# Inputs of a spectral mixer made chunk by chunk inside the attention ahead of it

## The chip, the cores and the metric

The kernel runs on one core of a Trainium2 chip. The metric is device time in microseconds (us) of one execution, the median of several runs. Profile times are us from the start of the profiled execution's span.

## The reference, cut to what matters

The network has four layers over 2 batches of L = 56·56 = 3136 tokens with C = 128 channels, all float32. Layers 0 and 1 are selective scans. The change lies in layer 2, which adds an attention without a token's own key, and then a spectral mixer; both read a layer norm of the tokens t.

```python
t = t + attn(_ln_t(t))                      # softmax(q q^T / sqrt(128)), diagonal masked
t = t + mix(_ln_t(t), sigma, phi, M_u, M_phi_plus, M_phi_minus, log_weights, gumbel)
t = t + attn3(_ln_t(t)); t = t + experts(_ln_t(t))          # layer 3

def mix(x, ...):                            # x: (2, 3136, 128)
    outs = []
    for i, frac in enumerate((1, 2, 4, 8)):
        xi = x[:, :T // frac]
        si = spectral(xi, sigma, phi, M_phi_plus[i], M_phi_minus[i]) + ar(M_u[i], xi)
        outs.append(pad(si, T))
    w = one_hot(argmax(y)) - y + y          # y = softmax(log_weights + gumbel), 4 values
    return sum(outs[i] * w[i])

def ar(Mu, u):                              # the direct part: three lags
    return sum(shift(u, i) @ Mu[i] for i in range(3))
# spectral: 16 causal convolutions of u with the filters phi, for u and for u with
# alternating signs; each result times sigma^0.25 and a 128x128 matrix, summed
```

## The kernel before, in words

Tokens stand in SBUF as X, 112 tokens of a tile on the partitions, 28 tiles, 2 batches. A chunk (CH = 448) is four such tiles; there are 7 a batch and 14 in all. Layers 0 and 1 run in an order written out by hand. Everything behind them is ordered by a list scheduler, which lists each engine's instructions from the program's dependences; instructions then run in that order on each engine's queue. DMAs are issued by SyncE (SP), in order. Pools decide where a tile lies, and a tile placed where another was waits for the other's last reader.

**Attention 2** (`Attention2.run`, which calls `Attend.run`). Its keys, queries and values are made during the tail of layer 1. For each chunk of queries it steps j over 25 tiles of keys: a matmul for the scores (L1031, tile sc), the exponential on ScalarE (L1033, e), their sum over tiles on GpSimd (L1044, total), and two steps behind, the product with the values (L1025, av). At the chunk's end av is copied (L1056, by), turned by four matmuls (L1060), and added to X divided by the sum of weights (L1067, L1070). `Attend.run` calls a hook `also(at, j)` in each step; attention 3 uses it to make its own inputs, attention 2 passes none.

**The mixer** (`layer2_mixer`, `Mixer`). Its convolutions are products of blocks of 128 tokens. It wants tokens backward, and even and odd tokens apart: tile x is 128 partitions × 13 blocks × both batches' channels, for one parity. So behind attention 2 it

1. computes the routing weights wt and ws from four numbers (L1487 to L1514), some 25 small instructions;
2. makes U, the layer norm of all of X, in four pieces (`layernorm_all`, L77 to L84);
3. reverses the 28 tiles' tokens by matmuls with a reversed identity `anti` (L1529, prv), copies them out (r) and stores them in a DRAM array `back` (L1532);
4. sums the matrices M_u by the routing weights to wu (`stretch_sums`, L1616 and L1618), turns U into channels uT (L108, pt) and computes the direct part into A by three matmuls for each of 8 segments of 392 tokens a batch (L1546, par);
5. loads the filters' taps H (L1366) and windows wA to wD (L1376), and in `Mixer.inputs` the blocks x from `back` with strided rows (L1320, L1322), and forms differences of blocks t, vA, vC and vD on VectorE (L1326 to L1357), with the tiles u0 and S as scratch;
6. runs 32 units. Each has convolution products (L1397, tile cv), of which ScalarE copies (L1412) or VectorE adds (L1410) the results into u0, u1 and S, and projections with matrices Wm (L1582, pj), added to A with a stride of two tokens (L1588). Between units 16 and 17 `Mixer.inputs` is called for the other parity.

**Attention 3** is built ahead of the mixer: five small loads (Wq, Wk, Wv, bq, bv) and a chain of small matmuls and VectorE copies make its constants (L1137 to L1148).

Of the kernel before, what the change touches and what calls it, by code (L numbers as in the profile page):

```python
# [14 lines left out]
F32 = mybir.dt.float32  # L15
BF16 = mybir.dt.bfloat16
AF = mybir.ActivationFunctionType
# [4 lines left out]
B = 2  # L22
# [97 lines left out]
class Scans:  # L120
# [177 lines left out]
    def run(self):  # L298
        with ExitStack() as ctx:
            self.open(ctx)  # L300
            with self.k.tc.manual_schedule():
                self.all_steps()
# [770 lines left out]
class Attention2:  # L1073
# [26 lines left out]
            k.evacuate(self.uT[b][:, CH * c : CH * (c + 1)], pt)  # L1100
            key_tiles(k, bank(self.pp, "pt"), self.uT[b], self.V[b], c)

    def run(self, early):
        k = self.k
        with k.pool("a2") as sp:
            skip = sp.tile([KT, KT], F32, name="skip")
            k.nc.vector.tensor_scalar(skip, k.ident, -1.0, 1.0, ALU.mult, ALU.add)
            done = early()
            with ExitStack() as ctx:
                Attend(k, ctx).run(self.uT, self.uT, self.V, 128.0**-0.5, k.ident, skip=skip)  # L1110
        return done


# [117 lines left out]
HL = L // 2  # L1231
REST = HL - KB * NB
PW = KB + HL + 16

# [48 lines left out]
    return raw, win  # L1285


class Mixer:


# [3 lines left out]

    def __init__(self, k, ctx, back, raw, win):
        self.k, self.back, self.raw, self.win = k, back, raw, win
        sp = ctx.enter_context(k.pool("mixx", 1))
        self.wp = ctx.enter_context(k.pool("mixw", 1))  # L1300
        self.cp = ctx.enter_context(k.pool("mixc", 1))
        self.p1 = ctx.enter_context(k.pool("pconv", 6, psum=True))

        self.x = sp.tile([KB, NB + 1, B * C], F32, name="x")
        k.nc.gpsimd.memset(self.x[:, NB, :], 0.0)
        self.sp = sp
        self.H = self.wp.tile([KB, 2, 2, HL], F32, name="H")
        self.W, self.waiting = {}, None

    def inputs(self, par):  # L1310

        nc, x, back = self.k.nc, self.x, self.back

        def rows(r0, n, more):
            return bass.AP(back.tensor, back.offset + r0 * B * C, [[2 * B * C, n], *more, [1, B * C]])

        for j in (8, 4, 0, NB):
            r0 = L - 1 - 2 * (KB * (NB - j) - 1) - par
            if j < NB:
                nc.sync.dma_start(x[:, j : j + 4, :], rows(r0, KB, [[2 * KB * B * C, 4]]))  # L1320
            else:
                nc.sync.dma_start(x[KB - REST :, NB, :], rows(0 if par else 1, REST, []))  # L1322
        self.v = {f"x{i}": x[:, NB - 1 - i, :] for i in range(NB)}

        def less(out, a, b):
# [143 lines left out]
        self.waiting = None  # L1469


def layer2_mixer(k, d, A, raw, win):

    nc, tc, X = k.nc, k.tc, k.X
    NF = 16
    QC = HL // 4  # L1480
    with ExitStack() as ctx:
        sp = ctx.enter_context(k.pool("m2", 1))

        lw = sp.tile([128, 4], F32, name="lw")
        gu = sp.tile([128, 4], F32, name="gu")
        sg = sp.tile([128, NF], F32, name="sg")
        nc.sync.dma_start(lw, d["L2_log_weights"].partition_broadcast(128))  # L1487
        nc.sync.dma_start(gu, d["L2_gumbel"].partition_broadcast(128))
        nc.sync.dma_start(sg, d["L2_sigma"].partition_broadcast(128))
        nc.scalar.activation(sg, sg, AF.Sqrt)  # L1490
        nc.scalar.activation(sg, sg, AF.Sqrt)
        s = sp.tile([128, 4], F32, name="s")
        nc.vector.tensor_add(s, lw, gu)
        mx = sp.tile([128, 1], F32, name="mx")
        nc.vector.tensor_reduce(mx, s, AX.X, ALU.max)
        nc.vector.tensor_scalar(s, s, mx, None, ALU.subtract)
        nc.scalar.activation(s, s, AF.Exp)
        nc.vector.tensor_reduce(mx, s, AX.X, ALU.add)
        nc.vector.reciprocal(mx, mx)
        nc.vector.tensor_scalar(s, s, mx, None, ALU.mult)  # L1500
        nc.vector.tensor_reduce(mx, s, AX.X, ALU.max)
        hard = sp.tile([128, 4], F32, name="hard")
        nc.vector.tensor_scalar(hard, s, mx, None, ALU.is_equal)
        free = sp.tile([128, 1], F32, name="free")
        nc.gpsimd.memset(free, 1.0)
        for i in range(4):
            nc.vector.tensor_mul(hard[:, i : i + 1], hard[:, i : i + 1], free)
            nc.vector.tensor_sub(free, free, hard[:, i : i + 1])
        wt = sp.tile([128, 4], F32, name="wt")
        nc.vector.tensor_sub(wt, hard, s)  # L1510
        nc.vector.tensor_add(wt, wt, s)
        ws = sp.tile([128, 4, NF], F32, name="ws")
        for i in range(4):
            nc.vector.tensor_scalar_mul(ws[:, i, :], sg, wt[:, i : i + 1])  # L1514

        dp = ctx.enter_context(tc.tile_pool(name="m2d", bufs=1, space=bass.MemoryType.DRAM))
        back = dp.tile([L, B, C], F32, name="back")
        with k.pool("m2u", 1) as up, k.pool("m2b", 3) as bp, k.pool("pm2", 2, psum=True) as pp:
            U = up.tile([TP, NT, B, C], F32, name="U")
            layernorm_all(k, U)  # L1520
            anti = up.tile([TP, TP], F32, name="anti")
            nc.gpsimd.memset(anti, 0.0)
            nc.gpsimd.affine_select(
                out=anti, in_=anti, pattern=[[1, TP]], compare_op=ALU.not_equal, fill=1.0, base=1 - TP,
                channel_multiplier=1,
            )
            for j in range(NT):
                ps = pp.tile([TP, B * C], F32, name="prv")
                nc.tensor.matmul(ps, lhsT=anti, rhs=U[:, j].rearrange("p b c -> p (b c)"), start=True, stop=True)  # L1529
                r = bp.tile([TP, B * C], F32, name="r")  # L1530
                k.evacuate(r, ps)
                nc.sync.dma_start(back[L - TP * (j + 1) : L - TP * j].rearrange("p b c -> p (b c)"), r)  # L1532

            mu = up.tile([128, 4, 3, C], F32, name="mu")
            nc.sync.dma_start(mu, d["L2_M_u"].rearrange("i s d e -> d i s e"))
            wu = up.tile([128, 4, 3, C], F32, name="wu")
            stretch_sums(nc.vector, wu, mu, lambda i: wt[:, i : i + 1])
            uT = up.tile([128, 2 + L], F32, name="uT")
            for b in range(B):
                nc.gpsimd.memset(uT[:, 0:2], 0.0)  # L1540
                tokens_to_channels(k, pp, lambda c0: uT[:, 2 + c0 : 2 + c0 + CH], lambda j: U[:, j, b, :])
                for t0 in range(0, L, QC):
                    r = stretch(t0)
                    ps = pp.tile([128, QC], F32, name="par")
                    for lag in range(3):
                        nc.tensor.matmul(  # L1546
                            ps, lhsT=wu[:, r, lag, :], rhs=uT[:, 2 + t0 - lag : 2 + t0 - lag + QC],
                            start=lag == 0, stop=lag == 2,
                        )
                    k.evacuate(A[:, b, t0 : t0 + QC], ps)  # L1550

        mixer = Mixer(k, ctx, back, raw, win)
        tp = ctx.enter_context(k.pool("tmix", 1))
        wp = ctx.enter_context(k.pool("wmix", 4))
        p2 = ctx.enter_context(k.pool("pproj", 2, psum=True))
# [53 lines left out]
def stretch(t0):  # L1609

    return 0 if t0 < L // 8 else 1 if t0 < L // 4 else 2 if t0 < L // 2 else 3


def stretch_sums(engine, out, m, weight):

    engine.tensor_scalar_mul(out[:, 3], m[:, 0], weight(0))  # L1616
    for i in range(1, 4):
        engine.scalar_tensor_tensor(out[:, 3 - i], m[:, i], weight(i), out[:, 4 - i], ALU.mult, ALU.add)  # L1618
# [233 lines left out]
def program(tc, d, out):  # L1852
    with ExitStack() as ctx:
        k = Chip(ctx, tc)
        dp = ctx.enter_context(tc.tile_pool(name="m2t", bufs=1, space=bass.MemoryType.DRAM))
        with k.pool("big") as bp:
            big = [bp.tile([128, NKT * C if i in (3, 5) else L], F32, name=f"big{i}") for i in range(6)]
            attention = Attention2(k, big)
            with ExitStack() as ctx1:
                heads = []  # L1860

                def follow(ctx):
                    heads.append(Layer1(k, ctx1, d, big))
                    return heads[0].start(ctx)

                layer0(k, d, big, follow)
                heads[0].run(attention.start)
            taps = attention.run(lambda: mixer_filters(k, d, dp))
        with ExitStack() as ctx3:
            attention = Attention3(k, ctx3, d)  # L1870
            A = ctx3.enter_context(k.pool("mixed")).tile([128, B, L], F32, name="A")
            layer2_mixer(k, d, A, *taps)
            attention.run(A)
        layer3_experts(k, d, out)

# [16 lines left out]
```

## Time and the profile before

| | us |
|---|---|
| median of three runs | 9403.43 (9399.32 to 9412.42) |
| the profiled execution | 9399.84 |
| its span | 9398.0 |
| PE busy in the span | 8136.1 (87%) |
| DVE busy | 7072.4 (75%) |
| POOL busy | 6320.6 (67%) |
| ACT busy | 3832.5 (41%) |

In the profile PE is TensorE's matmuls, PEld its weight loads, DVE VectorE, ACT ScalarE, POOL GpSimd. A row of the timeline has start, duration, engine, line, operation, out<-in, shapes and count, and in brackets the idle time before it and what ended it. A row of a group has busy time and mean ns of one behind the first bar, idle time and its releasers behind the second. A float32 matmul mostly appears as two records, a transpose as one. Attention 2 fills 6070 to 6633, the convolutions run from 6768 to about 8500, attention 3 to 9153, and the experts to the end.

### The profile page before, as it was taken

To read this page: it belongs to the slowest core of one execution; us is meant where nothing else is said; L and a number is where in the kernel's file an instruction comes from. 1 tells how busy PE (TensorE), PEld (TensorE's weight loads), DVE (VectorE), ACT (ScalarE), POOL (GpSimd) and SP (SyncE) were. 2 spreads that over 40 slices of the span, in tenths; PEclk is the share of its full clock that TensorE was granted. 3 is DMA by queue.
4 is the path that set the end of the run, shared out by engine and by line. 5 is a ranking of instruction groups with operands and counts; after the bars stand their busy time and mean duration, and the time that the engine had idled before them with its cause. 6 is when DMAs were issued, how large, how long until landed. Compare 5 with 4: busy or idle time off the path is not lost. (4 is left out here: it accounts for less than half of the span.)

```text
span 9398.0 us, 94099 instructions
## 1 busy us (share of the span) xinstructions
PE 8136.1 (87%) x28803; PEld 4794.3 (51%) x28803; DVE 7072.4 (75%) x7442; ACT 3832.5 (41%) x6517; POOL 6320.6 (67%) x4006
## 2 busy tenths in 40 slices
PE   7888888888888888888888888699799999999997
PEld 3444445444444444444444444355488888874545
DVE  8999998999996997997898799600467676665432
ACT  4555545555545555554555555233211111114331
POOL 5999997999995996997899699666211111115550
PEclk9999999999999998998999899699899999999998
DMA  5666664666663884885787588100233333310004
GB/s 156 221 221 216 213 202 136 220 221 215 214 202 104 223 214 121 223 219 146 193 218 202 141 223 213 51 1 1 73 95 107 101 104 94 105 53 1 1 12 147
DMA packets 800676, 1367.59 MB, mean 146 GB/s; under 512 B 125373, under 2 KB 434366, under 8 KB 800138
## 3 DMA queue, kind: packets, MB, share of 16 engines
q1 hardware_dynamic: 800170, 1361.57, 50.3%
q8 instruction: 228, 3.74, 0.2%
q14 instruction: 278, 2.28, 0.1%
HBM read 1320.14 MB, written 41.11 MB: 145 GB/s over the span
## 5 line engine op out<-in xcount | busy, mean ns | idle before, releaser
L423 POOL TENSOR_TENSOR p<-h,c 128x784 f32<-128x784 f32 x2048 | 3759.6, 1860 | 234.5 <-PE acc L371 158.1
L371 PE MATMUL acc<-p,ident 128*128 128x392 f32 x8192 | 3127.5, 513 | 87.4 <-POOL p L423 85.8
L351 DVE TENSOR_TENSOR_SCAN h<-a,state,h 128x784 f32<-128x784 f32 x1536 | 2798.5, 1842 | 88.5 <-ACT a L332 74.0
L371 PEld LDWEIGHTS acc<-p,ident 128*128 128x128 f32 x8192 | 1517.8, 197 | 1175.3 <-POOL p L423 199.5
L410 DVE TENSOR_TENSOR h<-du,b 128x784 f32<-128x784 f32 x1408 | 1336.4, 949 | 176.8 <-PE b L357 174.8
L332 ACT ACTIVATE a<-delta,L0A 128x784 f32<-128x784 f32 x1024 | 939.3, 919 | 836.7 <-DVE h L351 835.0
L426 POOL TENSOR_TENSOR h<-du,b 128x784 f32<-128x784 f32 x640 | 1189.6, 1859 | 3.1 <-DMA b<-rows 3.1
L357 PE MATMUL b<-three,sel 96*128 96x512 bf16 (+1 forms) x2816 | 709.2, 333 | 550.3 <-DVE h L410 509.7
L332 ACT ACTIVATE a<-delta,L1A 128x784 f32<-128x784 f32 x1024 | 937.3, 918 | 534.3 <-DVE h L351 531.9
L1044 POOL TENSOR_TENSOR total<-total,e 128x448 f32<-128x448 f32 (+1 forms) x644 | 729.9, 1133 | 322.3 <-ACT e L1033 294.5
L351 DVE TENSOR_TENSOR_SCAN h<-a,h 128x784 f32<-128x784 f32 x512 | 902.0, 1780 | 40.2 <-ACT a L332 32.3
L1441 POOL TENSOR_TENSOR u<-u,S 128x1024 f32<-128x1024 f32 x64 | 150.1, 2368 | 1136.2 <-DVE S L1410 1136.2
L1410 DVE TENSOR_TENSOR u<-u,cv 128x512 f32<-128x512 f32 x1024 | 623.4, 682 | 342.9 <-PE cv L1397 341.6
L357 PEld LDWEIGHTS <-sel 96*128 96x128 bf16 x2816 | 275.8, 98 | 1158.8 <-issue 921.9
L1033 ACT ACTIVATE e<-sc 128x448 f32<-128x448 f32 (+1 forms) x700 | 380.8, 544 | 788.8 <-PE sc L1031 611.1
L1412 ACT COPY u<-cv 128x512 f32<-128x512 f32 x256 | 149.6, 587 | 849.5 <-PE cv L1397 775.1
L1582 PE MATMUL pj<-u,Wm 128*128 128x196 f32 (+8 forms) x1536 | 351.4, 381 | 5.7 <-DVE A L1588 5.7
L1056 DVE COPY by<-av 128x448 f32<-128x448 f32 x28 | 17.5, 625 | 440.7 <-PE av L1025 440.7
L1031 PE MATMUL sc<-big 128*128 128x448 f32 (+1 forms) x700 | 323.8, 548 | 12.5 <-ACT e L1033 12.5
L385 PE MATMUL acc<-big,ident 128*128 128x392 f32 x384 | 250.6, 784 | 92.3 <-ACT big L391 92.3
L1031 PE MATMUL sc<-q,u 128*128 128x448 f32 (+1 forms) x700 | 323.0, 546 | 0.2 <-DVE q L984 0.2
L1025 PE MATMUL av<-e,big 128*128 128x448 f32 (+1 forms) x700 | 320.7, 544 | 1.1 <-DVE e L1038 1.1
(394 smaller groups left out, 10706.5 us busy)
## 6 DMA issues: line engine op xcount, KB each, us to landing
c<-rows SPq DMA_DIRECT2D x1024, 392.0 KB, 4.0
c<-rows SPq DMA_DIRECT2D x2048, 196.0 KB, 4.4
b<-rows SPq DMA_DIRECT2D x320, 392.0 KB, 4.5
b<-rows SPq DMA_DIRECT2D x640, 196.0 KB, 4.4
H<-raw SPq DMA_DIRECT2D x32, 1568.0 KB, 6.6
wC<-win SPq DMA_DIRECT2D x64, 576.0 KB, 5.9
wA<-win SPq DMA_DIRECT2D x64, 384.0 KB, 5.5
wD<-win SPq DMA_DIRECT2D x64, 320.0 KB, 4.4
```

The lines of the kernel that those rows point to most:

```text
L332: self.k.nc.scalar.activation(x["a"], g["delta"][ci], AF.Exp, scale=self.w["A"](g["kd"], ci, x["n"]))
L351: self.k.nc.vector.tensor_tensor_scan(h, a, h, start, ALU.mult, ALU.add)
L357: self.k.nc.tensor.matmul(ps[:, c0:c1], lhsT=self.w["selB"](x["n"]), rhs=x["g"]["three"][:, c0:c1], start=True, stop=True)
L371: nc.tensor.matmul(job["acc"][:, i, 0:392], lhsT=self.k.ident, rhs=x["p"][:, 392 * i : 392 * (i + 1)], start=False, stop=n == NS - 1,)
L410: nc.vector.tensor_tensor(one["h"], one["g"]["du"][one["ci"]], one["b"], ALU.mult)
L423: nc.gpsimd.tensor_tensor(now["p"], now["h"], now["c"], ALU.mult)
L426: nc.gpsimd.tensor_tensor(three["h"], three["g"]["du"][three["ci"]], three["b"], ALU.mult)
L1031: nc.tensor.matmul(ps[:n], lhsT=keys[b][:, KT * j : KT * j + n], rhs=q, start=True, stop=True)
L1033: nc.scalar.activation(e[:n], ps[:n], AF.Exp, scale=scale)
L1044: nc.gpsimd.tensor_tensor(total[:n], total[:n], e[:n], ALU.add)
L1410: nc.vector.tensor_tensor(place(o), place(o), ps, ALU.add)
L1582: nc.tensor.matmul(ps[:, lo - c0 : hi - c0], lhsT=Ws[f][:, eo, r, :], rhs=u[:, b, f, lo - a0 : hi - a0], start=f == 0, stop=f == 1,)
```

## The change

The mixer's inputs are made chunk by chunk in attention 2's hook. A new class `MixerInputs` holds the pools, the routing weights, wu, tile x and a DRAM array `odd`. It is constructed ahead of attention 2, so the weights and wu come there. For the chunk of queries finished before, the hook calls four steps during the next chunk:

- at j = 4 `tokens`: the layer norm of the chunk's four tiles (Um);
- at j = 11 `channels`: four transposes and one VectorE copy which reads the result backward, so uT holds channels with the tokens reversed;
- at j = 14 `blocks`: for each parity, transposes of every second column of uT, 128 tokens a block. Even blocks are copied into x; odd ones into a tile r (two buffers), and from there into DRAM `odd`, 64 KB a store, 26 stores;
- at j = 18 `direct`: three matmuls per segment (60 in all) on reversed channels, and a copy into A that reads backward.

The last chunk's four steps stand behind attention 2. `Mixer.inputs` loads nothing for even tokens, and x from `odd` in four loads for odd ones. The layer norm of all tokens, the `anti` matmuls, the array `back` and the loads from it are gone. uT lies in a tile `pair`, which takes the places of two tiles of layers 0 and 1. A and the new tiles are taken from the other side of SBUF, and attention 3's constants are built once the tiles of layers 0 to 2's attention are released. The bodies of `products`, `into`, `unit`, `project` and the rest of `Mixer` stay as they are.

```diff
-    def run(self, early):
+    def run(self, early, inputs):
         k = self.k
-        with k.pool("a2") as sp:
+        done = early()
+        with k.pool("a2") as sp, ExitStack() as ctx:
...
-            done = early()
-            with ExitStack() as ctx:
-                Attend(k, ctx).run(self.uT, self.uT, self.V, 128.0**-0.5, k.ident, skip=skip)
+            att = Attend(k, ctx)
+
+            def also(at, j):
+                steps = {4: inputs.tokens, 11: inputs.channels, 14: inputs.blocks, 18: inputs.direct}
+                if at > 0 and j in steps:
+                    steps[j](lambda: att.bank("lo"), *divmod(at - 1, NCH))
+
+            att.run(self.uT, self.uT, self.V, 128.0**-0.5, k.ident, skip=skip, also=also)
+            for step in (inputs.tokens, inputs.channels, inputs.blocks, inputs.direct):
+                step(lambda: att.bank("lo"), B - 1, NCH - 1)
         return done
...
+class MixerInputs:
+    T0 = 2 * KB * (NB + 1) - 1
+    def __init__(self, k, ctx, early, d, A, uT):
+        sp = ctx.enter_context(k.pool("mixx", side="right"))
+        self.up = early.enter_context(k.pool("mixu", 2, side="right"))
...
+        self.odd = dp.tile([KB, NB + 1, B * C], F32, name="odd")
         self.x = sp.tile([KB, NB + 1, B * C], F32, name="x")
-        k.nc.gpsimd.memset(self.x[:, NB, :], 0.0)
+        nc.gpsimd.memset(uT[:, 0 : self.T0 + 1 - L], 0.0)
+        nc.gpsimd.memset(uT[:, self.T0 + 1 :], 0.0)
...
+    def tokens(self, bank, b, c):
...
+        layernorm_tokens(self.k, self.U, self.k.X[:, 4 * c : 4 * (c + 1), b, :], sq, st, C)
+
+    def channels(self, bank, b, c):
+        k = self.k
+        ps = bank()[:, 0:CH]
+        for i in range(4):
+            k.nc.tensor.transpose(ps[:, TP * i : TP * (i + 1)], self.U[:, i, :], k.ident[:TP, :TP])
+        end = self.T0 + 1 - CH * c
+        k.nc.vector.tensor_copy(self.uT[:, end - CH : end], ps[:, ::-1])
+
+    def blocks(self, bank, b, c):
+        k, nc = self.k, self.k.nc
+        i0, i1 = CH * c // (2 * KB), NB + 1 if c == NCH - 1 else CH * (c + 1) // (2 * KB)
+        for par in range(2):
+            ps = bank().rearrange("p (i c) -> p i c", c=C)
+            for i in range(i0, i1):
+                at = self.T0 - 2 * KB * (i + 1) + 2 - par
+                nc.tensor.transpose(ps[:, i - i0, :], self.uT[:, at : at + 2 * KB - 1 : 2], k.ident)
+            for i in range(i0, i1):
+                j = NB if i == NB else NB - 1 - i
+                if par == 0:
+                    k.evacuate(self.x[:, j, C * b : C * (b + 1)], ps[:, i - i0, :])
+                else:
+                    r = self.up.tile([KB, C], F32, name="r")
+                    k.evacuate(r, ps[:, i - i0, :])
+                    nc.sync.dma_start(self.odd[:, j, C * b : C * (b + 1)], r)
+
+    def direct(self, bank, b, c):
+        k, nc = self.k, self.k.nc
+        ps = bank()
+        edges = sorted({CH * c, CH * (c + 1)} | {t for t in (L // 8, L // 4, L // 2) if CH * c < t < CH * (c + 1)})
+        for t0, t1 in zip(edges, edges[1:]):
+            for lag in range(3):
+                end = self.T0 + 1 - t0 + lag
+                nc.tensor.matmul(
+                    ps[:, CH * (c + 1) - t1 : CH * (c + 1) - t0], lhsT=self.wu[:, stretch(t0), lag, :],
+                    rhs=self.uT[:, end - (t1 - t0) : end], start=lag == 0, stop=lag == 2,
+                )
+        nc.vector.tensor_copy(self.A[:, b, CH * c : CH * (c + 1)], ps[:, 0:CH][:, ::-1])
...
     def inputs(self, par):
...
-        for j in (8, 4, 0, NB):
-            r0 = L - 1 - 2 * (KB * (NB - j) - 1) - par
-            if j < NB:
-                nc.sync.dma_start(x[:, j : j + 4, :], rows(r0, KB, [[2 * KB * B * C, 4]]))
-            else:
-                nc.sync.dma_start(x[KB - REST :, NB, :], rows(0 if par else 1, REST, []))
+        if par:
+            for j in (8, 4, 0, NB):
+                js = slice(j, min(j + 4, NB + 1)) if j == NB else slice(j, j + 4)
+                nc.sync.dma_start(x[:, js], self.odd[:, js])
...
+                    A = ctx3.enter_context(k.pool("mixed", side="right")).tile([128, B, L], F32, name="A")
+                    with ExitStack() as early:
+                        given = MixerInputs(k, ctx2, early, d, A, pair[:, 0:MU])
+                        taps = attention.run(lambda: mixer_filters(k, d, dp), given)
+                attention = Attention3(k, ctx3, d)
+                layer2_mixer(k, d, given, *taps)
```

## The prediction

> **What bounds the kernel now.** I read the page's rows of busy time and slices first (TensorE 87%, VectorE 75%), then the busy time by stretch around the change. The columns are PE, PEld, DVE, ACT, POOL, the granted clock, the DMA share and GB/s.
>
> ```profile
> 6100.00:6640.00 540.00, 534.55 (x1561) 270.98 (x1559) 48.12 (x147) 181.51 (x334) 360.63 (x323) 0.99 0.01 2
> 6640.00:6660.00 20.00, 4.59 (x18) 3.27 (x18) 19.56 (x31) 7.47 (x9) 6.32 (x2) 0.59 0.02 6
> ...
> 6700.00:6720.00 20.00, 19.76 (x81) 12.37 (x80) 5.32 (x10) 3.96 (x8) 2.81 (x3) 1.00 0.26 76
> 6720.00:6740.00 20.00, 8.25 (x26) 4.40 (x24) 1.14 (x2) 1.46 (x3) 0.00 (x0) 0.82 0.54 188
> 6740.00:6760.00 20.00, 7.25 (x25) 6.08 (x26) 8.96 (x14) 0.00 (x0) 0.00 (x0) 0.58 0.76 204
> 6760.00:6780.00 20.00, 12.30 (x46) 10.11 (x45) 12.24 (x19) 3.81 (x7) 0.00 (x0) 0.74 0.00 1
> 6780.00:6800.00 20.00, 20.00 (x95) 17.65 (x94) 17.14 (x29) 2.93 (x5) 1.24 (x1) 1.00 0.44 105
> ```
>
> Attention 2 (to 6640) is bound by PE: 534.55 of 540 us busy, with VectorE at 9%, ScalarE at 34%, GpSimd at 67%. From 6780 the mixer is bound by PE too. Between them no engine leads for long: normalization on DVE, then reversal and direct part on PE, then loads and sums. The timeline gives that gap its ends and its last steps.
>
> ```profile
> 6632.90 0.60 DVE L1070 SCALAR_TENSOR_TENSOR X<-pr,r,X 112x128 f32<-112x128 f32 x2
> ...
> 6750.93 0.43 DVE L1330 SCALAR_TENSOR_TENSOR t<-x 128x256 f32<-128x256 f32 x1 [24.05 <-DMA x<-back]
> ...
> 6767.88 0.68 DVE L1326 TENSOR_TENSOR vD<-S 128x512 f32<-128x512 f32 x1
> 6768.05 2.05 ACT L1412 COPY u<-cv 128x512 f32<-128x512 f32 x4 [39.28 <-DVE vD L1326]
> ```
>
> X is final at 6633.50, and the convolution stream runs from 6768.05, when ScalarE may write u0, the scratch of the vD sums. So 134.6 us lie between: to 6728.8 for making U, its reversal and the direct part, to 6750.9 for the loads (x last), 17.1 us for sums on DVE.
>
> **The change, part by part.** *The gap goes.* Only the last chunk's steps stay behind attention 2. Normalizing four tokens' columns took about 5.7 us in attention 3 (DVE 0.69, 0.16, 0.68, ACT 0.63, DVE 0.67, a table load of 1.28, 0.30, DVE 0.20, POOL 1.04, the queue order being the same); then transposes 0.6, reversed copy 0.6, six block transposes and copies about 2, three direct matmuls 2.3: 11.2 us, to about 6644.7. Attention 3's constants now come here. The load of Wq waits on SP for memory that the last direct matmul reads, so about 6646, and the taps H and windows wA to wD are queued behind it. Before, 7.7 MB landed in 22.6 us (6728.3 to 6750.9: 343 GB/s); without x it is about 6.0 MB, 17.5 us, so about 6664. DVE needs 17.1 us from 6645 for t and the v tiles, and its copies of Wq, Wk, M, Mb and vb stand between these and wait for PE (that chain took 6.4 us before, 6631.9 to 6638.3; I add 4): 6666. Both paths meet at about 6666, 32.5 us after X. Saved: 134.6 − 32.5 = **102 us**. The reversed copy has no row as a copy; the scans of line 351, half of which read backward, have minimum, median and maximum of 1822, 1844 and 1868 ns, so I charge a plain copy.
>
> *Attention 2 gets longer, since PE has no idle time there.* These rows size what it gains:
>
> ```profile
> L1546 PE MATMUL par<-uT,wu 128*128 128x392 f32 x96 | 35.7, 512 | 0.0
> L1529 PE MATMUL prv<-U,anti 112*112 112x256 f32 x56 | 22.4, 510 | 28.8 <-DVE r L64 15.5 <-POOL U L84 12.9 <-ACT r L68 0.4
> ...
> L108 PE MATMUL pt<-ident,U 112*128 112x112 f32 x56 | 9.1, 300 | 0.9 <-ACT uT L68 0.9
> ```
>
> The 48 direct matmuls of 392 columns took 35.7 us, 0.74 each; one of 448 in attention's steady pace takes 0.75. For each of 13 chunks: three direct, 2.25; four transposes, 0.60 (the row of line 1207 below); 46 block transposes over 13 chunks at 0.15 each, 0.53. That is 3.38 × 13 = 44 us, and 1 for chunks cut at 392, 784 and 1568. Block transposes read every second column: no row has that for a transpose. The nearest are the accumulations of line 385, at stride 56, 784 ns against 513 in line 371, so the 46 cost between nothing and 4 more (7 if they double). I take nothing. The multiplications by `anti` (22.4 us) fall away inside the gap and are not counted again.
>
> Each chunk also inserts a Sqrt among ScalarE's exponentials. Attention 3 already does so:
>
> ```profile
> 8594.16 1.28 ACT L82 ACT_TABLE_LOAD   x1
> 8595.46 0.30 ACT L82 ACTIVATE st<-st,eps 112x4 f32<-112x4 f32 x1
> 8595.77 1.28 ACT L1033 ACT_TABLE_LOAD   x1
> 8597.07 0.55 ACT L1033 ACTIVATE e<-sc 128x448 f32<-128x448 f32 x1
> ...
> 8597.21 0.60 PE L1207 MATMUL pr<-ident,U 112*128 112x112 f32 x4 [0.69 <-POOL U L84]
> ```
>
> From the load to the next exponential's end is 3.46 us, and PE lost 0.69, not to ScalarE but to U. In attention 2 the queue has scores made ahead, and I count 3.0 us of PE work before PE needs that exponential, against 3.46 less the overlap in which it starts early: 0 to 0.7 a chunk, I take 0.5, so 6 us. A rule speaks against this. The Trainium skill, "ScalarE: Activation LUTs", section "What ACT_TABLE_LOAD costs", adds about 1380 ns of drain to the 1283 ns, 2.66 us a switch. The rows have the 1283 and no drain: 8594.16 + 1.28 meets the Sqrt at 8595.46. By the rule, two switches take 2.76 us more, 13 times: 36 us more, and the gain would shrink to about 9. I keep the row. Attention 2: **+51 us** (42 to 87 between the ends).
>
> Other engines: normalization, the reversed copies and block copies add some 6 us a chunk to DVE (9% busy), 3 of copies and squares to ScalarE (34%), 1 to POOL (67%). PE covers them; if it did not, a chunk would lose what DVE or POOL is late, 1 to 3 us, 13 to 39 in all. The 26 stores of odd blocks have SP to themselves; with two r buffers the third in a row waits for a landing, 2.4 us by the median of back<-r, off PE's path unless an exponential stands behind it.
>
> *The routing weights and wu move ahead of attention 2*, into layer 1's tail: 27 more DVE instructions. Their price depends on GpSimd:
>
> ```profile
> 6647.56 0.16 DVE L1507 TENSOR_TENSOR hard<-hard,free 128x1 f32<-128x1 f32 x1
> ...
> 6647.85 3.02 DVE L1508 TENSOR_TENSOR free<-free,hard 128x1 f32<-128x1 f32 x1
> ```
>
> Alone it is 0.16 us, beside a long multiply of POOL 3.02. In the tail small DVE instructions had means of 0.2 to 0.86, and DVE was busy 99.74 of 151 us, with one idle stretch of 7.7 us for PE. 23 small ones at 0.35 are 8, four wu 2.4 to 7.2; half lies in idle time: **+5** (−5, when they fill waits and the order shifts, to +16). With them go four loads on SP (three small ones, and mu with 786 KB, issued during a scan) and two short memsets on POOL: I count nothing; if the scan's next rows waited behind mu, 3 us.
>
> *Odd tokens at the half-way switch*: x comes from a different array in as many loads of the same bytes: nothing, ±2. *Projection weights* now load behind wD and may be late for the first projection: **+1** (0 to 8).
>
> The sum: −102 + 51 + 5 + 1 = **−45**, on the profiled execution's 9399.84: 9354.8. The median of the runs is 3.6 higher; carried over, 9358. I say 9357.
>
> **The rivals.** *Table switches stall PE.* As worked out, 36 us more: 9393, no change that shows. For it: attention 2 has 1.60 us a step against 1.9 in attention 3, so less cover. Against: no drain in the rows.
>
> *The start of the stream gives it back.* H waits behind Wq, which waits for the last direct matmul and for room; if H, windows and projection weights come one after another with DVE's copies waiting for PE, the stream starts 15 to 25 us later: about 9378. For it: SP is one queue, in order. Against: bytes at 343 GB/s don't need it.
>
> *Slower: layer 1's tail.* Each of the 27 DVE instructions is caught behind a POOL multiply of 2 to 3 us, in the stretch 5919 to 6070, where DVE leads into attention 2. At 3.02 each it is 82 us where I have 5: +32, 9434. It breaks even at 50 us, 1.85 each, and shows as slower from about 2.5 each. For it: the row above, and POOL busy 87.5 of those 151 us. Against: the tail's own small ones averaged under 0.9.
>
> *The change does not do what it says*: a scheduler could leave the hooks' steps behind attention. The order of the instructions shows them inside, so little is left to this: 9400.
>
> **How the numbers follow.** The sum as worked out 0.73; table switches 0.09 (9393); late stream 0.10 (9378); slower tail 0.05 (9434); no effect 0.03. The likeliest gives 9357. The unknowns of the sum (+36 or −9 in attention 2, ±10 in the tail, ±8 at the start) spread it over about 9328 to 9380, and the late stream and part of the switches bring the upper end to 9395. About 0.2% (18.8 us) is what a measurement here can tell from no change: faster takes the first case and most of the late stream, 0.83; same the switches, no effect and edges, 0.11; slower 0.06.
>
> **What would show it.** Right: chunks of attention 2 (starts of line 1056) about 43.5 us apart, not 40; PE waiting under 1 us a chunk; the first u copy about 33 us after X's last update; small DVE instructions before attention 2 under 1 us, and its first exponential near 6075, not 6070. Wrong: chunks of 46 or more with PE waiting for e; H issued well after the last direct matmul, or PE idle 50 us behind attention; attention 2 starting 30 us or more later.

## The result, and the profile after

Three jobs compared the changed kernel with the kernel before. The ratios are 0.9936 (95% interval 0.9919 to 0.9953; medians 9345.87 and 9406.91 us), 0.9945 (0.9932 to 0.9959) and 0.9949 (0.9937 to 0.9962): faster by 0.5 to 0.6%, 49 to 61 us between medians. The profiled execution took 9347.92 us with a span of 9345.7, 52 us less than before.

Busy time by stretch, with the columns of the prediction's first fence:

```profile
6100.00:6640.00 540.00, 539.90 (x1659) 280.38 (x1658) 99.40 (x233) 213.74 (x382) 354.57 (x312) 1.00 0.01 3
6640.00:6680.00 40.00, 39.01 (x120) 19.86 (x118) 5.36 (x15) 15.46 (x28) 26.24 (x24) 1.00 0.01 4
6680.00:6700.00 20.00, 9.45 (x25) 5.61 (x26) 13.17 (x29) 3.01 (x6) 1.23 (x2) 0.60 0.19 55
6700.00:6720.00 20.00, 17.61 (x70) 14.52 (x70) 14.41 (x24) 3.81 (x7) 0.26 (x1) 0.81 1.04 303
6720.00:6740.00 20.00, 16.94 (x64) 13.71 (x63) 13.29 (x25) 2.93 (x5) 7.22 (x6) 0.83 0.53 138
6740.00:6760.00 20.00, 20.00 (x127) 18.71 (x127) 18.16 (x32) 0.37 (x1) 6.29 (x4) 1.00 0.36 93
```

Attention 2 now fills PE wholly, and lasts longer. From 6680 to 6740 PE is idle for 16 of 60 us; before, it was short of work from 6640 to 6780, but for the direct part in between. The timeline shows the same steps as before:

```profile
6679.98 1.13 DVE L1070 SCALAR_TENSOR_TENSOR X<-pr,r,X 112x128 f32<-112x128 f32 x4
...
6694.65 0.62 DVE L1398 COPY A<-lo 128x448 f32<-128x448 f32 x1 [1.05 <-PE lo L1394]
...
6695.19 0.41 DVE L1434 SCALAR_TENSOR_TENSOR t<-x 128x256 f32<-128x256 f32 x1
...
6703.52 1.19 PE L1501 MATMUL cv<-H,t 128*128 128x256 f32 x2 [2.39 <-DMA H<-raw]
...
6710.60 0.68 DVE L1430 TENSOR_TENSOR vD<-S 128x512 f32<-128x512 f32 x1
6710.77 2.05 ACT L1516 COPY u<-cv 128x512 f32<-128x512 f32 x4 [18.27 <-DVE vD L1430]
```

X is final at 6681.11, and the stream runs from 6710.77: 29.7 us, where it was 134.6. And what PE does for the mixer inside attention 2, from the groups of 6110 to 6660:

```profile
L1394 PE MATMUL lo<-pair,wu 128*128 128x448 f32 (+5 forms) x108 | 29.9, 422 | 0.0
...
L1377 PE MATMUL lo<-ident,pair 128*128 128x128 f32 x46 | 7.5, 280 | 0.0
L1365 PE MATMUL lo<-ident,Um 112*128 112x112 f32 x52 | 7.1, 259 | 0.0
```

In all three the idle time before them is zero, and PE is busy for 539.90 of 540 us: no new wait of any size stands in front of it. Five marks, the same in every kernel, cut the span into stages. "Tail" runs from the end of the last scan to attention 2's first exponential; "clock-up" from there to the first copy of av; then to X's last update; to the first u copy; and to the copy of `rest`, which ends the first unit. All in us, from one trace each:

| trace | last scan ends | tail | clock-up | attention 2 | gap | first unit | span behind the scan |
|---|---|---|---|---|---|---|---|
| before | 5919.9 | 150.1 | 39.7 | 523.8 | 134.6 | 43.9 | 3478.1 |
| before, again | 5916.4 | 151.1 | 39.7 | 523.8 | 134.6 | 43.6 | 3478.7 |
| changed | 5922.2 | 153.7 | 39.7 | 565.5 | 29.7 | 48.3 | 3423.5 |
| changed, 2nd | 5921.5 | 155.2 | 42.0 | 565.4 | 29.8 | 48.3 | 3429.0 |
| changed, 3rd | 5928.2 | 154.1 | 42.2 | 565.5 | 29.9 | 46.5 | 3426.9 |
| all steps behind | 5934.2 | 155.2 | 42.0 | 524.0 | 95.7 | 45.3 | 3448.1 |
| no direct part | 5927.3 | 160.5 | 39.7 | 535.1 | 27.6 | 44.3 | 3393.3 |
| switch at the rule's price | 5919.7 | 150.6 | 42.3 | 598.9 | 31.6 | 43.4 | 3454.3 |
| taps first | 5926.5 | 155.2 | 42.0 | 565.4 | 41.9 | 48.0 | 3441.2 |
| weights held back | 5933.2 | 152.8 | 41.6 | 567.5 | 27.5 | 46.6 | 3424.3 |
| late, weights held | 5917.5 | 152.8 | 41.5 | 560.9 | 26.0 | 47.6 | 3417.3 |
| late | 5928.4 | 155.4 | 41.9 | 556.6 | 26.0 | 46.6 | 3417.1 |

From the means of two and three traces: tail +3.7, clock-up +1.6, attention 2 +41.7, gap −104.8, first unit +4.0, what is left +2; together −52.

### The profile page after: what moved, and what is told of

It is laid out like the page before. It is cut to its first block, busy times and chain, and to the rows that moved or that the text cites. A ratio compares the mean times of both kernels' runs of the same rounds, so it can differ in the third digit from the quotient of the medians.

```text
span 9345.7 us, 94244 instructions
## 1 busy us (share of the span) xinstructions
PE 8131.6 (87%) x28823; PEld 4793.0 (51%) x28823; DVE 7098.7 (76%) x7517; ACT 3857.7 (41%) x6560; POOL 6325.3 (68%) x4013
## 4 chain that ended last, share of the span: by engine, by line
PE 49%; DVE 21%; issue 12%; ACT 9%; POOL 4%; DMA 4%; SPq 1%; DVEq 0%; POOLq 0%; ACTq 0%
PE cv L1501 12%; DVE h L351 10%; PE acc L371 7%; DVE h L410 7%; PE av L1025 6%; PE sc L1031 6%; PE pj L1615 4%; ACT a L332 3%; PE b L175 3%; PE acc L385 2%; DMA c<-rows 2%; POOL p L423 2%; DMA whole<-rows 1%; PE pcv L452 1%; PE b L357 1%
## 5 line engine op out<-in xcount | busy, mean ns | idle before, releaser
L1545 POOL TENSOR_TENSOR u<-u,S 128x1024 f32<-128x1024 f32 x64 | 150.1, 2366 | 1043.3 <-DVE S L1514 1043.3
L1025 PE MATMUL av<-e,V 128*128 128x448 f32 (+1 forms) x700 | 320.8, 545 | 0.0
L970 DVE TENSOR_REDUCE m<-lo 112x1 f32<-112x448 f32 x392 | 227.2, 618 | 119.0 <-PE lo L966 118.6
```

The lines of the kernel that those rows point to most:

```text
L1025: nc.tensor.matmul(acc, lhsT=V[b][:n, j, :], rhs=e[:n], start=j == 0, stop=j == NKT - 1)
```

## The experiments

**How large is it?** The changed kernel once more, in two jobs, and the kernel before for a second trace.

> The changed kernel as it is, against the kernel before. Two readings of the size: the two profiled executions differ by 52 us (9399.8 to 9347.9, ratio 0.9945), all of it in named stages; the medians of the four runs differ by 61 us (ratio 0.9935). Theory one: the 52 us of the stages are the change, and the other 9 us are scatter of the runs of the kernel before; then this ratio is 0.994 to 0.995. Rival: the change is worth 61 us or more and the profiled execution of before was a lucky one: 0.993 to 0.9938.

> The kernel before once more, for a second trace. Theory: the scatter of single executions (9396 to 9422 us) sits in layers 0 and 1, where five traces with the same order of instructions end the last scan between 5919.7 and 5934.2; behind it the stages repeat: 150 us from the last scan to the first exponential of attention 2, 523.8 from the first copy of av to X's last update, 134.6 to the first u copy, within 1 us each. Rival: the stages of the change scatter too, and the gains read from one pair of traces are uncertain by more than 5 us.

> The changed kernel on the same chip as the version above, for a comparison in one job. Theory: stages behind the last scan 3423 to 3429 us again, ratio to the kernel before 0.994 to 0.995.

Measured: 0.9945 (0.9932 to 0.9959) and 0.9949 (0.9937 to 0.9962); the traces are in the table. The first theories hold in the main: attention 2 and the gap repeat within 0.3 us between traces of one kernel, while the end of the last scan moves by 18 us between traces whose instructions up to there have one order, but for two short ones of the routing weights. So the 52 us of the stages are the change. The 9 us that the first job's medians show beyond that are within the scatter of its runs (9399.32 to 9412.42 before); where they lie is not shown, since those runs have no trace. "Within 1 us each" holds for the kernel before, but is too strong for tail, clock-up and first unit of the changed one, which move by 1.5 to 2.5 us.

**Is it the method or the hiding?** All 14 chunks' steps behind attention 2:

```diff
             def also(at, j):
-                if at > 0 and j in steps:
-                    steps[j](lambda: att.bank("lo"), *divmod(at - 1, NCH))
+                return
...
-            for step in (inputs.tokens, inputs.channels, inputs.blocks, inputs.direct):
-                step(lambda: att.bank("lo"), B - 1, NCH - 1)
+            for at in range(B * NCH):
+                for step in (inputs.tokens, inputs.channels, inputs.blocks, inputs.direct):
+                    step(lambda: att.bank("lo"), *divmod(at, NCH))
```

> The hook does nothing; all 14 chunks' four steps stand behind attention 2. Theory: attention 2 returns to 40.0 us a chunk (42 us less), and the steps take what their busiest engine takes: DVE some 4.8 us a chunk (layer norm 2.4, reversed copy 0.62, copy to A 0.62, block copies 1.1), 67 us, and 12 to fill and drain. From X's last update to the first u copy about 29 + 65 = 95 us, the total 20 to 25 us above the changed kernel. So most of the gain (134.6 to 95) comes from how the inputs are made and only some 23 us from hiding them. Rival: hiding is what pays; unhidden the new steps cost as much as the old ones, 130 us or more from X to u, and the total is near or above the kernel before, 55 us above the changed one.

Measured: 9384.41 us in one run; attention 2 524.0, gap 95.7 us; behind the last scan 21.6 us above the changed kernel's mean of 3426.5. Of the 104.8 us that the gap lost, 38.9 come from how the inputs are made (no reversal by matmuls, no trip of x through DRAM ahead of the first product, and routing weights and wu made in layer 1's tail; these three were not measured apart) and 65.9 from hiding. Hiding is paid for in attention 2 with 41.7, which leaves 24.2. So the first theory holds, with its sizes: net, 39 us are the method's and 24 the hiding's, less what tail, clock-up and first unit give back.

**Does PE's work in attention 2 cost its full time?** The direct part is left out:

```diff
     def direct(self, bank, b, c):
         k, nc = self.k, self.k.nc
-        ps = bank()
+        nc.gpsimd.memset(self.A[:, b, CH * c : CH * (c + 1)], 0.0)
+        return
```

> The direct part's matmuls and their copies into A are left out (A is set to zero on GpSimd instead), all else stays. Theory: attention 2 has no idle PE time, so each chunk gets shorter by what they take, 2.25 us: from the first to the last copy of av 561.6 becomes about 532, and the last chunk's chain loses 4.5 us: total about 34 us less. Rival: they lie partly in time in which PE would have waited for ScalarE or GpSimd (total at 1.13 us a step of 1.6, e): 10 us or less.

Measured: 9322.45 us; attention 2 535.1, 30.3 less, or 2.33 for each of 13 chunks. It is the full price of the matmuls; the rival's 10 us falls. (The tail is 6 us longer here. The scheduler is free to put the 14 memsets into it; that they are the cause was not tested.)

**What would the drain have cost?** One long ScalarE instruction, `idle`, behind each Sqrt, and a one-column Sqrt that it waits for:

```diff
         layernorm_tokens(self.k, self.U, self.k.X[:, 4 * c : 4 * (c + 1), b, :], sq, st, C)
+        nc, ident = self.k.nc, self.k.ident
+        two = self.up.tile([TP, 1], F32, name="two")
+        nc.scalar.activation(two, sq[:, 0, 0:1], AF.Sqrt, bias=self.k.eps[:TP], scale=1.0 / C)
+        idle = self.up.tile([TP, 24, C], BF16, name="idle")
+        nc.scalar.activation(idle, ident[:TP].unsqueeze(1).to_broadcast([TP, 24, C]), AF.Identity, bias=two)
```

> One ScalarE instruction of about 2.75 us (a broadcast copy that nobody reads) stands behind each Sqrt in attention 2, ahead of the table load for the next exponential: the price that the drain rule would have put on the two switches. Theory: in the changed kernel the exponential behind the switches ends 0.1 us ahead of the matmul that needs it, so the whole 2.75 us becomes PE time, 13 times: 35 us from the first to the last copy of av (561.6 to about 597), and the total as much. Rival: scores made ahead and ScalarE's 60% of idle time absorb it: under 10 us.

Measured: 9375.79 us; attention 2 598.9 us, 33.4 more, 2.57 a chunk for an instruction of 2.84. First come ScalarE's rows and the matmul that needs the exponential in the changed kernel's timeline, and then the same place here:

```profile
6295.85 0.53 ACT L1033 ACTIVATE e<-sc 128x448 f32<-128x448 f32 x1
...
6296.39 1.28 ACT L82 ACT_TABLE_LOAD   x1
...
6297.69 0.30 ACT L82 ACTIVATE stm<-stm,eps 112x4 f32<-112x4 f32 x1
...
6298.00 1.28 ACT L1033 ACT_TABLE_LOAD   x1
...
6299.30 1.47 ACT L1033 ACTIVATE e<-sc 128x448 f32<-128x448 f32 x3
6299.96 0.95 PE L1025 MATMUL av<-e,big 128*128 128x448 f32 x2
```

The first of the three exponentials, of 0.55 us, ends at 6299.85, and the matmul that reads it starts at 6299.96 without a wait. With the instruction in between:

```profile
6306.14 2.84 ACT L1364 ACTIVATE idle<-ident,two 112x3072 bf16<-112x3072 f32 x1
...
6309.00 1.28 ACT L1033 ACT_TABLE_LOAD   x1
...
6310.30 1.42 ACT L1033 ACTIVATE e<-sc 128x448 f32<-128x448 f32 x3
6310.92 1.00 PE L1025 MATMUL av<-e,big 128*128 128x448 f32 x2
```

So the margin in the changed kernel is 0.1 us, as the expectation had it. It is so in most chunks; in two it is 0.9, and in one the matmul waited 0.1. From the first table load to the exponential's start the path is 2.9 us longer here (5.84 against 2.91), and PE pays 2.57 of that in the mean. Single chunks lost 1.6 to 3.8 us, since the scheduler also placed the hook's matmuls anew, so the size is that of the whole edit. An estimate from it: had each switch a drain as the rule says, the change would have kept some 19 of its 52 us.

**Do the loads set the start of the stream?** Taps and windows issued ahead of attention 3's constants (a method `constants`, called as `between`, now holds the loads and the chain):

```diff
         mixer = Mixer(k, ctx, given, raw, win)
+        for eo in range(2):
+            mixer.taps(0, eo)
+        for name in SUMS:
+            mixer.windows(name, 0, 0)
+        between()
```

> Taps H and windows are issued ahead of attention 3's constants on SP, whose loads no longer stand before them; projection weights are issued earlier too. H moves from 13.4 us behind the last update's end of X (6696.8 less 6681.1 is 15.7) to about 12. Theory: VectorE's chain (block copies, 17 us of sums, five copies of constants) sets the start of the stream, so the first u copy stays at 29 to 31 us behind X. Rival: the loads set it: the first u copy comes 3 to 6 us earlier, 24 to 27.

Measured: 9369.67 us, and both miss: the gap grew to 41.9 us. SP's and PE's rows of that timeline:

```profile
6704.11 7.42 SPq L1486 DMA_DIRECT2D wB<-win  x2
...
6717.48 1.00 SPq L1146 DMA_DIRECT2D L3Wq<-in_L_Wq_dram  x1
...
6722.49 0.47 PE L1151 MATMUL Wq<-ident,L3Wq 128*128 128x128 f32 x1 [19.78 <-DMA L3Wq<-in_L_Wq_dram]
...
6727.15 1.22 PE L1507 MATMUL cv<-H,t 128*128 128x256 f32 x2 [0.38 <-DVE vb L1164]
```

VectorE was through with vD at 6717.29, 28.2 us behind X, so it was on time for the theory. But PE runs in order, and the constants' chain stands ahead of the first product. Its loads now came behind the taps and windows, and SP took 16 us to issue those (two of wB alone 7.42). The order that the change has, small loads first, is the better one of the two.

**What do the routing weights cost in layer 1's tail?** The 27 VectorE instructions held back to attention 2's second chunk by adding zero times the first chunk's copy of av:

```diff
+                if at == 1 and j == 6:
+                    inputs.weights(att.by)
...
         nc.vector.tensor_add(s, lw, gu)
+        nc.vector.scalar_tensor_tensor(s, by[:, 0:4], 0.0, s, ALU.mult, ALU.add)
```

> The 27 instructions of the routing weights and wu are held back by a term of value zero from the first chunk's copy of av, so that they run in attention 2's second chunk on an idle VectorE. From the last scan to the first exponential it was 150.1 before, and 153.7, 155.2, 150.6 and 155.2 in four traces with these instructions in layer 1's tail. Theory: they cost up to 5 us there by delaying the norms' small instructions, and now it is 150 to 151; attention 2 stays at 565.5. Rival: the tail scatters by itself by 5 us, whatever stands in it: anything from 150 to 155.

Measured: 9359.34 us; tail 152.8, attention 2 567.5. Inconclusive for the tail: 152.8 lies between the 150.1 and 151.1 of before and the 153.7 to 155.2 of the changed kernel, and the trace with the longer ScalarE instruction has 150.6 with the same tail as the changed kernel. What it did show is a price on the other side: attention 2's second chunk took 45.4 us, not 43.3. There the weights stood ahead of the mask multiplications on VectorE's queue (next experiment's row). The gap, whose instructions the edit leaves alone, was 27.5 us; the part on the prediction comes back to that.

**A version drawn from these.** Direct parts of the last five chunks behind attention 2, where PE idles, and ScalarE copying them to A; attention 3's constants made during the mixer's fifth unit; pools of the projection weights opened ahead of the mixer's. Once with the weights held back, once without:

```diff
-                if at > 0 and j in steps:
+                if at > 0 and j in steps and (j != 18 or at - 1 < 9):
                     steps[j](lambda: att.bank("lo"), *divmod(at - 1, NCH))
...
+            for c in range(2, NCH):
+                inputs.direct(lambda: att.bank("lo"), B - 1, c, k.nc.scalar.copy)
...
-        mixer = Mixer(k, ctx, given, raw, win)
         tp = ctx.enter_context(k.pool("tmix", 1))
         wp = ctx.enter_context(k.pool("wmix", 4))
+        mixer = Mixer(k, ctx, given, raw, win)
...
+            if n == 4:
+                constants(lambda: p2.tile([128, 512], F32, name="pj"))
```

> A version drawn from the runs. Routing weights held back into attention 2 as in the run with the weights; the direct parts of the last five chunks stand behind attention 2, where PE idles, with ScalarE copying them to A; attention 3's constants are made during the mixer's fifth unit; the pools of projection weights are opened first, so that what waits for the channels' memory is needed late. Theory: four direct parts less in attention 2, 4 times 2.3 is 9 us (565.5 to 556); the gap from X to the first u copy loses VectorE's copies of constants, 29.7 to about 27; up to 4 us in layer 1's tail; total 12 to 15 us below the changed kernel, ratio to before 0.993. Rival: PE in the gap is needed by the first products, the direct parts delay the stream by what they take, 9 us, and the total is that of the changed kernel.

> As the version drawn before, but with the routing weights left in layer 1's tail, since held back into attention 2 they stood ahead of the mask multiplications on VectorE and cost PE 4.6 us there. Theory: from the first copy of av to X's last update 565.4 less 4 times 2.3, 556.2 us; from there to the first u copy 26; the tail 150.6 to 155.2 as in the changed kernel; 12 to 15 us below the changed kernel behind the last scan. Rival: the deferred direct parts cost elsewhere what they save, and the stages behind the last scan sum to the changed kernel's 3423 to 3429.

Measured: ratio to the kernel before 0.9937 (0.9923 to 0.9951) with the weights held back and 0.9929 (0.9915 to 0.9943) without; in the job of the latter the changed kernel had 0.9949 (0.9937 to 0.9962), medians 9341.31 and 9357.30. Behind the last scan they take 3417.3 and 3417.1 us, 9 less than the changed kernel's mean. A chunk without its direct part took 40.9 us, not 43.15, and the gap fell to 26.0 although five direct parts now stand in it. So the rivals fall in the stages, while the forecasts of 12 to 15 us miss and the intervals of the whole still overlap. Part of it is given back: the unit with the constants took 104.4 us against 102.7 for the others. The first of the two lost time in its second chunk, by this group of that chunk and the 4 us behind its wait:

```profile
L1025 PE MATMUL av<-e,big 128*128 128x448 f32 (+1 forms) x50 | 24.4, 581 | 1.7 <-DVE e L1038 1.7
```

```profile
6126.72:6130.72 4.00, 4.00 (x6) 2.00 (x7) 0.14 (x1) 0.00 (x0) 3.68 (x4) 0.57 0.01 2
```

PE waited 1.7 us for masked exponentials, was then granted 0.57 of its clock for 4 us, and the chunk took 47.75 us; in the version without held weights it took 43.30. In the run that only held the weights back the same wait of 1.7 us left the clock at 1.00, and the chunk lost 2.1 us instead of 4.5. Why the clock fell in one and not in the other is not shown.

## Why the prediction was right, point by point

The prediction said 9357 us, 46 below the median of before, and faster; measured were 49 to 61 us. Its sum was −45, the stages give −52: attention 2 is 9 us better than costed, the gap 3 and the tail 1, and the first unit, clock-up and the rest are some 7 worse.

*The gap* was costed at −102 and is −104.8. The chain ran as written down: 5.3 us of norm to U, transposes, copy, blocks, and VectorE's sums with the constants' copies between them. H's landing held the first product for 2.4 us and lay beside VectorE's work. VectorE's last sum released the first u copy, as said. But PE's clock has a part in it that the prediction left out: among its sums VectorE waited 1.9 us for PE, 1.05 of it for the direct part. The gap of the changed kernel, and of the run with held weights:

```profile
6681.11:6710.77 29.66, 17.82 (x51) 12.01 (x52) 22.29 (x41) 3.01 (x6) 1.23 (x2) 0.61 0.51 164
```

```profile
6694.98:6722.53 27.55, 14.43 (x48) 9.60 (x48) 22.14 (x42) 3.00 (x6) 1.23 (x2) 0.69 0.50 166
```

With 0.69 of the clock instead of 0.61 the last direct part took 3.36 us instead of 4.49, VectorE did not wait for it, and the stream started 2.1 us earlier. So the 26.0 us of the last version, whose gap had 0.77, may not all be its edit.

*Attention 2* was costed at +51 and is +41.7. The step that was mis-sized is the stall behind the table switches, 0.5 us a chunk and 6 in all. It is 0.1 in all: PE was busy 539.90 of 540 us. With a margin of 0.1 us, that is close to luck. (PE's missing 5 us in the fence of before were no idle time to fill: with all steps behind attention 2 it is busy for 540.00 of 540 us at the same 39.99 us a chunk.) Besides, the added work was taken as 3.38 us a chunk and is 3.2 (41.7 over 13): 2.33 for the direct part and its cuts by the run without it, the rest for transposes and blocks. (The busy times of the three groups above add up to 44.5 us, 2.8 more than the stage grew; where that went is not shown.) The block transposes over every second column took 280 ns for 128 columns, the plain ones 259 for 112, so no cost of the stride shows, the end that was chosen. The reversed copy, too, took what the plain copy of av takes:

```profile
6677.23 0.62 DVE L1056 COPY by<-av 128x448 f32<-128x448 f32 x1 [1.80 <-PE av L1025]
...
6687.52 0.62 DVE L1367 COPY pair<-lo 128x448 f32<-128x448 f32 x1 [2.29 <-PE lo L1365]
```

*The rule that was weighed against it*, the drain of about 1.38 us in the Trainium skill's "ScalarE: Activation LUTs", section "What ACT_TABLE_LOAD costs", does not show in this case: in the changed kernel's fence of that experiment the loads of 1.28 us meet their neighbours within 0.02 us at both ends. Keeping the row was right, and it mattered, since the margin was 0.1 us.

*Layer 1's tail* was costed at +5 and is +3.7 (2.6 to 5.0 between single traces). The rival on the slower side had its mechanism, but seldom. From the timelines of the two engines and the groups of the tail:

```profile
5920.09 5.46 POOL L423 TENSOR_TENSOR p<-h,c 128x784 f32<-128x784 f32 x3
...
5922.15 3.42 DVE L1328 TENSOR_TENSOR s<-lw,gu 128x4 f32<-128x4 f32 x1
...
5933.86 0.98 DVE L1343 TENSOR_TENSOR free<-free,hard 128x1 f32<-128x1 f32 x1
```

```profile
L1349 DVE TENSOR_SCALAR ws<-sg,wt 128x16 f32<-128x16 f32 x4 | 6.1, 1532 | 0.0
...
L1651 DVE SCALAR_TENSOR_TENSOR wu<-mu,wt,wu 128x384 f32<-128x384 f32 x3 | 1.8, 607 | 0.0
L1342 DVE TENSOR_TENSOR hard<-hard,free 128x1 f32<-128x1 f32 x4 | 0.6, 143 | 0.1
```

Some took 0.8 to 3.4 us beside GpSimd (the first one ended 0.02 us behind GpSimd's 5925.55), most ran in their 0.14 to 0.6: far below the 1.85 us each from which it would have decided. The prediction left out ScalarE's side: two more table loads of 1.28 us, for the weights' Sqrt and Exp, also stand in the tail. That the weights are the cause of the 3.7 us is not shown: in the two runs that held them and these loads back the tail was 152.8, still 2.2 above the mean of before, and the run with the longer ScalarE instruction had 150.6 with them in it. The sign "first exponential near 6075" came true at 6075.92, in part by luck, since the last scan ended 2.3 us later in that trace than in the one before.

*The first unit* is 4.0 us longer where +1 was forecast. Projection weights are late as feared: GpSimd waited 24.88 us for them, their sums on VectorE fell among the adds of u, and PE waited for those, 3.1 us in this unit.

```profile
6719.74 1.27 POOL L1595 TENSOR_TENSOR both<-mpm 128x512 f32<-128x512 f32 x1 [24.88 <-DMA mpm<-in_L_M_phi_minus_dram]
...
6730.87 1.27 PE L1501 MATMUL cv<-wC,vC 128*128 128x256 f32 x4 [2.35 <-DVE u L1514]
```

```profile
6768.05:6811.92 43.87, 43.23 (x221) 38.80 (x222) 30.77 (x51) 6.75 (x13) 4.70 (x2) 0.93 0.29 69
```

```profile
6710.77:6759.08 48.31, 45.25 (x228) 39.73 (x227) 35.64 (x63) 6.75 (x13) 12.85 (x9) 0.93 0.57 143
```

These are the unit before and after: PE is idle for 3.1 us, not 0.6, and busy for 2.0 more. So 2.4 of these 4.4 us are waits; the rest is open. That lateness is the cause was not tested alone: with the taps first the same weights came some 15 us earlier against the stream, PE was idle for 0.8 us, and the unit took 48.0 all the same, but with more of its products behind the mark that starts it.

*The half-way switch* to odd tokens took 115.9 to 117.0 us from copy to copy of `rest` against 115.7 and 115.8: 0.1 to 1.4 more, within the ±2 of the forecast.

## What to carry to other kernels

Work moved under a stage that one engine fills is not free: here the direct part cost that engine its time in full, so move what the full engine does least of and leave its matmuls where it idles. Before a step is put between another engine's regular instructions, count the margin to the next consumer; here 3.5 us of ScalarE just fitted, and 2.8 us more were paid nearly in full. When a queue is reordered, look at what waits for the one that now comes last: here five small loads behind some 6 MB of large ones cost 12 us.

## What was not expected of the hardware

Attention 2's start comes in two speeds, by the granted clock (the column ahead of the DMA share). The 5 us that begin 5 us behind the first exponential, in the changed kernel's first and second trace:

```profile
6080.92:6085.92 5.00, 4.94 (x13) 2.57 (x14) 1.36 (x3) 1.71 (x5) 4.46 (x4) 1.00 0.00 0
```

```profile
6081.66:6086.66 5.00, 5.00 (x7) 2.40 (x8) 1.35 (x2) 1.01 (x3) 4.33 (x4) 0.53 0.00 0
```

PE has the same work and is full in both, but the second got about half of the clock, and its first copy of av came 42.0 us behind the first exponential, not 39.7. In four of the twelve traces the full clock came 3.8 to 4.5 us behind that exponential, in the other eight 8.8 to 10.3 us, and those eight have the longer stage. What decides between them is not shown. The kernel before had the short one in both of its traces, so the 1.6 us of clock-up in the sum may be chance.

Of the scatter of whole executions a large part sits in the scans ahead of everything that was changed: the last one ended between 5916.4 and 5934.2 over all traces. Behind the scans the changed kernel's three traces still differ by 5.5 us.
